# Moving one group's norm at the head of two context attentions, and adding their output biases batch by batch

## The chip, the cores and the metric

The kernel runs on one core of one Trainium2 chip. Its time is the device time of one launch in microseconds (us). An engine works through its instructions in the order in which the program gives them; work on one engine waits for work on another through semaphores. The engines are named as the profile names them: PE (matrix multiplications and transposes), PEld (its weight loads), DVE and POOL (element-wise work), ACT (activations and copies), SP (issues transfers, written SPq).

## The reference, cut to what matters

The reference is a decoder of four layers on 16 batches of 112 rows and 256 columns, in f32. Each layer is an attention, a context attention over 375 rows of context, and a feed-forward part, each with a layer norm ahead and a residual addition behind:

```python
x = x + _L2_attn_ref(_layernorm(x, axis=-1), ...)
x = x + _L2_xattn_ref(ctx_1024, _layernorm(x, axis=-1), mask_BxSxS2_ik0, ...)   # layer 3's context attention
x = x + _L2_ffn_ref(_layernorm(x, axis=-1), ...)                                # experts, two of eight for each row
x = x + _L3_attn_ref(_layernorm(x, axis=-1), ...)                               # a whole block: attention, norm, MLP
x = x + _L3_xattn_ref(_layernorm(x, axis=-1), ctx_1024, ctx_1024, ...)          # layer 4's context attention
x = x + _L3_ffn_ref(_layernorm(x, axis=-1), ...)                                # ternary weights
```

In the reference and in the kernel the layers count from 0, so `l2` in a name is layer 3 and `l3` is layer 4. Both context attentions have 16 heads of 16 columns: a query projection, scores against the keys of the context, a softmax, values, an output projection with a bias, and the residual. Layer 3's also norms its projected queries and keys and has a mask; layer 4's has neither. The feed-forward part of layer 4 (`l3f`) makes its two weights ternary at run time: the mean of the absolute values of each weight is formed, and each entry becomes −1, 0 or 1 by half that mean.

## The kernel before

The program runs twelve phases in order, `l0_attn` to `l3_ffn`. The residual lies on chip throughout, as the tile `xres` (`K.x`), 112 rows x 16 batches x 256. Batches are taken in four groups of four (`NG`, `G4`; `GC` is 448, the rows of one group). A framework allots the tiles, sets the semaphores and orders the instructions of each engine: near neighbours in the source may change places, and the order of issue on each engine is then fixed.

Many helpers are generators: a phase interleaves them step by step, so that the work of one fills the gaps of another. `zip_steps` runs several in turn until all have ended. `ln_steps` norms one group of four batches: statistics on DVE (lines 180, 181), variance plus epsilon (160), the reciprocal root on POOL (166, tiles `rs_...`), four row norms on DVE (207, tiles `xn_...`), eight transposes on PE (148, `lnT_...`) and two copies from PSUM to the transposed group `xT`.

Layer 3's context attention is `l2_xattn`. Ahead of it, in `l2_attn`, the norm of each group (`l2x_norm`) is made when its last batch is done; the fourth group's can only follow the last batch, whose last residual addition is POOL's line 1556. Then `l2_xattn` folds the value bias into the output bias (`add_output_bias`: two-chunk product `bo_l2x` on PE, sum `bc_L2x_bo` on DVE at 1007, 16 additions to the residual on POOL at 1009), scales `wo` (1676), fetches two batches (`fetch`: keys `kT`, values `v`, mask `mi`, all by SP) and projects them (`project`: `l2x_q` on PE, `qn` and its statistics on DVE, `rs_l2x_q` on POOL, `qp` on DVE at 1706, copies `vp` of the values on POOL at 1708, the mask row `neg` on DVE at 1710, four transposes `l2x_qT`). After that a stream runs over 64 units, a unit being a batch and four of its heads: scores `ha_sl2x` on PE, maxima `e` and `mx` on DVE (1733), exponentials on ACT, transposes `l2x_t`, and values `l2x_o` of the unit before. The projection of batch b+2 is spread over the stream as `ahead`, one step in each unit.

Layer 4's self-attention is `l3_attn`. Its tail is the MLP of the last group: norm `l3ac`, hidden `l3a_m` (32 matmuls), output `l3a_d` (64 matmuls), added to the residual at line 223. Only then `l3_xattn` begins with its own bias row (`bo_l3x`) and `queries(0)`, which norms group 0, adds the bias to its four batches on POOL (2172) and makes the projections `l3x_q`. `spread` copies the values of a batch on POOL (2166). The stream again takes four heads a step, t from −5 to 64: scores `ha_sl3x`, maxima `mx` (2192); a batch's maxima are turned (`shift`, `l3x_m`, sum `q` at 2240) ahead of the second product `l3x_t`, the exponentials `e` and the values `l3x_o`. `queries` of the next group is spread over the stream. The list `others` holds work of the phase after: `l3f_weights`, which loads `w_L3f_fc` and `w_L3f_proj` and makes them ternary on DVE (sums at 2280, tests `lo` at 2294, 2295), one step in each t from t = −5 on.

Other parts that the change touches: `open_nx` opens the pools `nx` (the tile `l2x_xT`, the transposed norm of a whole phase) and `so` (tiles for sorting rows by expert), which `program` closes after `l3_attn`. `Sorted` loads a table of constants (`sort_cols`) and is made twice, in `l1_ffn` and `l2_ffn`. The pool `w` has six slots for weights, used in turn; SP waits with a load for the slot's last reader.

Of the kernel before, what the change touches and what calls it, by code (L numbers as in the profile page):

```python
# [10 lines left out]
F32 = mybir.dt.float32  # L11
# [3 lines left out]
ALU = mybir.AluOpType  # L15
# [4 lines left out]
B = 16  # L20
S = 112
D = 256
T = B * S
# [3 lines left out]
G4 = 4  # L27
NG = B // G4
GC = G4 * S
# [12 lines left out]
class Kern:  # L42
# [33 lines left out]
    def open_nx(self):  # L76


        self.l3pools = [self.tc.tile_pool(name=n, bufs=1) for n in ("nx", "so")]
        nx, self.so_pool = [p.__enter__() for p in self.l3pools]  # L80
        self.l2x_xT = nx.tile([128, 2, T], F32, name="l2x_xT")
        self.normed = None

    def open_l3c(self):

        pools = [self.tc.tile_pool(name=n, bufs=m) for n, m in (("l3c1", 1), ("l3c", 2))]
        self.l3pools += pools
        w1, wk = [p.__enter__() for p in pools]
        steps = l3x_context(self, w1, wk)
        self.l3x_fill = lambda: next(steps, steps) is not steps  # L90

# [1086 lines left out]
class Sorted:  # L1178
# [4 lines left out]
    def __init__(self, K, pool, E, name):  # L1183
        self.K, self.E, self.name = K, E, name
        self.NT = (2 * T + E * 127) // 128
        self.xd = K.dram.tile([T, D], F32, name=f"{name}_xd")
        self.ys = K.dram.tile([self.NT * 128, D], F32, name=f"{name}_ys")
        self.shapes = pool.tile([128, K.ins["sort_cols"].shape[1]], F32, name=f"{name}_shapes")
        K.nc.sync.dma_start(out=self.shapes, in_=K.ins["sort_cols"])

    def shp(self, name):
        a, n = SORT_AT[name]
# [264 lines left out]
def l2_attn(K):  # L1457
# [3 lines left out]
    nc, tc = K.nc, K.tc  # L1461
# [3 lines left out]
    with tc.tile_pool(name="l2a", bufs=2) as wk, tc.tile_pool(name="l2a1", bufs=1) as w1:  # L1465
# [113 lines left out]
        while todo or live:  # L1579
            if todo:  # L1580
                b = todo.pop(0)
                if b % G4 == 0:
                    zip_steps(ahead)
                    ahead = scores(b // G4 + 1) if b // G4 + 1 < NG else iter(())
                live.append((b, attend(b)))
                if b % 2:
                    K.l3x_fill()
            for n, item in enumerate(list(live)):
                if next(item[1], item) is item:
                    live.remove(item)  # L1590
                    if item[0] % G4 == G4 - 1:
                        norms.append(K.l2x_norm(wk, item[0] // G4))
                if n % 2 == 0:
                    next(ahead, None)
            if norms and next(norms[0], norms) is norms:
                norms.pop(0)
# [57 lines left out]
def l2_xattn(K):  # L1654
# [4 lines left out]
    nc, tc = K.nc, K.tc  # L1659
    wq = K.weight("L2x_wq", 2, D)  # L1660
    wo = K.weight("L2x_wo", 2, D)
    with tc.tile_pool(name="l2x", bufs=2) as wk, tc.tile_pool(name="l2x1", bufs=1) as w1:
# [5 lines left out]
        qps = padded_tiles(K, w1, [S], "qp")  # L1668
        xT = K.l2x_xT
        if K.normed is None:  # L1670
            for q in range(NG):
                zip_steps(K.l2x_norm(wk, q))
        K.normed = None
        add_output_bias(K, wk, wo, K.col("L2x_vb"), K.brow("L2x_bo"), "l2x")
        for kk in range(2):
            nc.vector.tensor_scalar(wo[:, kk, :], wo[:, kk, :], K.col("L2x_vs")[:, kk : kk + 1], None, ALU.mult)
        bq = K.brow("L2x_bq")
        qs, qb = K.col("L2x_qs"), K.col("L2x_qb")
        ready, fetched = {}, {}

# [13 lines left out]
        def project(b):  # L1694
# [13 lines left out]
                nc.gpsimd.tensor_copy(vp[:, c, :, :16], v[:, c])  # L1708
            neg = wk.tile([S, SK], F32, tag="mask_f", bufs=3, name=f"neg{b}")
            nc.vector.tensor_scalar(neg, mi, 0.0, NEG, ALU.is_equal, ALU.mult)  # L1710
            if b + 1 < B and b > 0:
                fetch(b + 1)
            yield
# [57 lines left out]
        units = [(b, g) for b in range(B) for g in range(4)]  # L1771
        maxima, exponentials = scores(*units[0])
        exponentials(maxima())
        ahead, behind = iter(()), []
        for k in range(len(units) + 1):
            more = scores(*units[k + 1]) if k + 1 < len(units) else None
            if k:
                b, g = units[k - 1]
                values(b, g)
                if g == 2 and b + 2 < B:  # L1780
                    ahead = project(b + 2)
                if g == 3:
                    behind.append(heads_steps(K, wk, pos[b], wo, K.x[:, b, :], f"l2x{b}", True))
# [125 lines left out]
def l3_attn(K):  # L1909
# [5 lines left out]
    with tc.tile_pool(name="l3a", bufs=2) as wk, tc.tile_pool(name="l3a1", bufs=1) as w1:  # L1915
# [183 lines left out]
            mlp_step()  # L2099
        while outs:  # L2100
            out_steps()
        for g in mlps:
            zip_steps(g)

# [29 lines left out]
def l3_xattn(K):  # L2136
# [8 lines left out]
    with tc.tile_pool(name="l3x", bufs=2) as wk, tc.tile_pool(name="l3x1", bufs=1) as w1:  # L2145
# [20 lines left out]
                nc.gpsimd.tensor_copy(vps[b % 2][:, c, :, :16], vs[b][:, c])  # L2166

        def queries(q):
            xT = wk.tile([128, 2, GC], F32, tag="xT", name=f"xT{q}")
            yield from K.ln_steps(wk, K.x, q, "l3x", xT=xT, bufs=1)  # L2170
            for b in range(q * G4, (q + 1) * G4):
                nc.gpsimd.tensor_tensor(K.x[:, b, :], K.x[:, b, :], bo[:S], ALU.add)
            yield
            qTs[q] = wk.tile([128, 4, GC], F32, tag="qT", name=f"qT{q}")
            for g in range(4):
                ps = K.bank(f"l3x_q{q}{g}")
# [43 lines left out]
        for b in range(3):  # L2220
            fetch(b)
        bo = K.brow("L3x_bo")
        add_output_bias(K, wk, wo, K.col("L3x_bv"), bo, "l3x", ())
        zip_steps(queries(0))
        for b in range(2):
            spread(b)
# [1 line left out]
        for t in range(-5, 4 * B + 1):  # L2228
# [13 lines left out]
            for item in list(behind):  # L2242
                if next(item[1], item) is item:
                    behind.remove(item)
                    if item[0] % G4 == G4 - 1:
                        others.append(K.l3f_left.pop(0))
            if others and next(others[0], others) is others:
                others.pop(0)
            if 0 <= t < 4 * B and s < 3:
                weights(b, s)  # L2250
# [359 lines left out]
def program(tc, ins, out, phases):  # L2610
    with ExitStack() as ctx:
# [4 lines left out]
        for phase in phases:  # L2616
# [27 lines left out]
                    zip_steps(l3x_context(K, w1, wk))  # L2644
            if phase in (l3_xattn, l3_ffn) and not hasattr(K, "l3f_left"):
                pool = ctx.enter_context(tc.tile_pool(name="l3f1", bufs=1))
                K.l3f_xT = pool.tile([128, 2, T], F32, name="l3f_xT")
                K.l3f_left = [l3f_weights(K, pool)] + [l3f_rows(K, pool, q) for q in range(NG)]
            phase(K)
            if phase is l3_attn:  # L2650
# [22 lines left out]
```

## Time and profile before

| what | value |
|---|---|
| median of 3 runs | 3657.05 us (3647.51 to 3661.35) |
| profiled execution | 3657.38 us, of which the span of the trace is 3655.6 us |
| mean granted clock of PE | 0.941 of full speed |
| layer 3's context attention, last `l2a_y` on PE to first scores | 2098.9 to 2135.8 us |
| layer 4's context attention, end of `l3a_d` to first maximum | 3249.1 to 3269.4 us |

Times in the trace are us from the span's start. In a timeline a line gives the start, the length, the engine, the line of the kernel, the operation, output<-input and count; the bracket is the idle time of the engine just before, and who ended it. A line of waits gives the waiting engine and tile, who released it, the total, the number of times, and the longest. Where several like instructions follow each other they are merged in one line with their busy time. A window gives the busy time of each engine in a stretch, the granted clock of PE (1.00 is full speed), the share of the 16 transfer engines in use and GB/s.

### The profile page before, as it was taken

The page shows a single profiled execution, that of the slowest core. Times are in us where ns is not written, and L with a number is a line of the kernel's source. Part 1 is how long each engine was busy: PE and PEld are TensorE (multiplying, and loading weights), DVE is VectorE, ACT ScalarE, POOL GpSimd, SP SyncE. Part 2 cuts the span into 40 slices and gives each one's busy share as a digit, 9 for nine tenths or more (in the row PEclk, how much of TensorE's full clock was granted, in tenths as well). Part 3 has the DMA queues.
Part 4 walks back from the last instruction along what each step waited for, and adds up shares of the span by engine and source line. Part 5 has one row for each costly group of instructions (what it writes and reads, how often), then busy time and mean ns, then how long its engine had stood idle before and what let it go on. Part 6 is the DMA issues. An engine that isn't in the chain of part 4 may idle for free. (4 is left out here: it accounts for less than half of the span.)

```text
span 3655.6 us, 72104 instructions
## 1 busy us (share of the span) xinstructions
PE 3242.1 (89%) x29426; PEld 2225.4 (61%) x29426; DVE 1961.5 (54%) x5065; ACT 1343.8 (37%) x2772; POOL 481.3 (13%) x636
## 2 busy tenths in 40 slices
PE   5999989789988898689978979989999979889999
PEld 2444444456756676457664547668889856656666
DVE  5766665363264454445435568872442286457754
ACT  2344444332233233112233347742222246714431
POOL 1000000020110000020142420001000132022110
PEclk9999999999989888888999979998999989979999
DMA  3021211510131211314182122137999710021200
GB/s 124 22 51 30 62 44 35 106 47 18 41 94 46 71 48 44 90 31 126 61 288 79 47 66 57 41 96 276 355 355 308 244 40 1 1 66 47 55 6 21
DMA packets 231275, 332.48 MB, mean 91 GB/s; under 512 B 109904, under 2 KB 183728, under 8 KB 215840
## 3 DMA queue, kind: packets, MB, share of 16 engines
q1 hardware_dynamic: 207392, 295.22, 26.8%
q0 software_dynamic: 6816, 17.57, 1.8%
q10 hardware_dynamic: 16736, 15.07, 1.3%
q8 instruction: 232, 3.80, 0.4%
q14 instruction: 99, 0.81, 0.1%
HBM read 270.53 MB, written 57.27 MB: 90 GB/s over the span
## 5 line engine op out<-in xcount | busy, mean ns | idle before, releaser
L1842 DVE SCALAR_TENSOR_TENSOR hT<-l2f_b,b,sl 128x128 f32<-128x128 f32 x280 | 94.8, 349 | 248.6 <-PE l2f_b L154 121.1
L1841 ACT ACTIVATE sl<-l2f_a,b 128x128 f32<-128x128 f32 x280 | 98.9, 366 | 292.4 <-PE l2f_a L154 222.4
L154 PE MATMUL l2f_a<-l2f_xT,w_L2f_w 128*128 128x128 f32 x1120 | 194.8, 288 | 5.4 <-DMA w_L2f_w<-in_L2f_w 4.5
L154 PE MATMUL l2f_b<-l2f_xT,w_L2f_w 128*128 128x128 f32 x1120 | 188.2, 282 | 1.9 <-DVE hT L1842 1.1
L154 PE MATMUL l0x_k<-w_L0x_wk,cT 128*125 128x512 f32 x384 | 179.6, 611 | 0.0
L154 PEld LDWEIGHTS l2f_a<-l2f_xT,w_L2f_w 128*128 128x128 f32 x1120 | 161.3, 192 | 29.4 <-ACT sl L1841 12.5
L154 PE MATMUL l0x_c<-kn,cx 125*128 125x512 f32 x384 | 178.9, 603 | 0.0
L1742 ACT ACTIVATE e<-e,mx 112x375 f32<-112x375 f32 x256 | 143.1, 607 | 54.6 <-DVE mx L1737 54.6
L303 DVE TENSOR_TENSOR pr<-qT,kT 128x576 f32<-128x576 f32 (+14 forms) x168 | 145.6, 898 | 30.0 <-PE l0a_s L306 23.8
L154 PEld LDWEIGHTS l2f_b<-l2f_xT,w_L2f_w 128*128 128x128 f32 x1120 | 152.9, 192 | 5.6 <-DVE hT L1842 4.8
L2192 DVE TENSOR_REDUCE mx<-ha_sl3x 112x1 f32<-112x375 f32 x256 | 121.9, 537 | 51.8 <-PE ha_sl3x L1017 51.7
L154 PE MATMUL l2f_d<-w_L2f_w,hT 128*128 128x256 f32 x560 | 144.2, 380 | 0.0
L1733 DVE CUSTOM_DVE_ANT_0 e<-ha_sl2x,neg 112x375 f32<-112x375 f32 x256 | 125.0, 544 | 16.3 <-PE ha_sl2x L1017 14.2
L154 PEld LDWEIGHTS l0x_k<-w_L0x_wk,cT 128*125 128x125 f32 x384 | 71.4, 192 | 93.0 <-issue 87.5
L154 PEld LDWEIGHTS l0x_c<-kn,cx 125*128 125x128 f32 x384 | 70.0, 190 | 92.7 <-issue 88.3
L2212 ACT ACTIVATE e<-l3x_t 125x448 f32<-125x448 f32 x192 | 88.8, 551 | 96.4 <-PE l3x_t L2207 96.4
L411 ACT ACTIVATE sq_k<-l0x_k 125x512 f32<-125x512 f32 x96 | 57.3, 597 | 130.7 <-PE l0x_k L154 130.4
L154 PEld LDWEIGHTS l2f_d<-w_L2f_w,hT 128*128 128x128 f32 x560 | 95.7, 191 | 7.2
L306 PE MATMUL l0a_s<-pr,R 128*32 128x448 f32 x672 | 93.7, 547 | 6.7 <-DVE pr L303 6.6
L148 PE MATMUL l2x_t<-ident,e 112*125 112x112 f32 x768 | 97.6, 277 | 1.4 <-ACT e L1742 1.3
L148 PEld LDWEIGHTS l2x_t<-ident,e 112*125 112x125 f32 x768 | 93.3, 192 | 7.2 <-ACT e L1742 2.9
L154 PE MATMUL l2x_kv<-w_l2x_kv,ctxT 128*125 128x512 f32 x192 | 96.3, 655 | 0.0
(785 smaller groups left out, 7193.0 us busy)
## 6 DMA issues: line engine op xcount, KB each, us to landing
w_L2f_w<-in_L2f_w SPq DMA_DIRECT2D x105, 1024.0 KB
ctxT<-in_ctxT SPq DMA_DIRECT2D x48, 375.0 KB
w_L1f_e<-in_L1f_e SPq DMA_DIRECT2D x43, 384.0 KB
a<-skew SPq DMA_DIRECT2D x32, 392.0 KB
cx<-in_ctx SPq DMA_DIRECT2D x16, 375.0 KB
l2x_v<-vo SPq DMA_DIRECT2D x16, 375.0 KB
l2x_kT<-kTo SPq DMA_DIRECT2D x16, 375.0 KB
c<-in_ctx SPq DMA_DIRECT2D x16, 375.0 KB
```

What stands on the lines that cost most here:

```text
L148: self.nc.tensor.transpose(out, in_, self.ident[:k, :k])
L154: self.nc.tensor.matmul(out, lhsT=l, rhs=r, start=i == 0, stop=i == n - 1)
L303: V.tensor_tensor(prs[j][:, :, :, off:], qT[q][:, :, :, off:], kT[q][:, :, :, : S - off], ALU.mult)
L306: nc.tensor.matmul(ps[32 * j : 32 * j + 32, :GC], lhsT=R[:, hf, 4 * c + j, x, :], rhs=prs[j][:, hf].rearrange("p b s -> p (b s)"), start=x ...
L411: nc.scalar.activation(sq[:p, n * 8 : n * 8 + 8, :], heads[n], AF.Square)
L1733: nc.vector.tensor_tensor_reduce(out=e[:, j, :], in0=banks[j][:S, :SK], in1=neg, scale=1.0, scalar=-3.0e38, op0=ALU.add, op1=ALU.max, accu ...
L1742: nc.scalar.activation(es[b, g][:, j, :], es[b, g][:, j, :], AF.Exp, bias=mx[:, 1, j : j + 1], scale=0.25)
L1841: nc.scalar.activation(sl, pa[:, at], AF.Silu, bias=b1[:, m + i : m + i + 1])
L1842: nc.vector.scalar_tensor_tensor(hT[:, m + i, :], pb[:, at], b1[:, 8 + m + i : 9 + m + i], sl, ALU.add, ALU.mult)
L2192: nc.vector.tensor_reduce(mxs[b][:, 4 * g + j : 4 * g + j + 1], ps[:S, :SK], AX.X, ALU.max)
L2212: nc.scalar.activation(es[b, c][:, j].rearrange("p g s -> p (g s)"), banks[j][:CK, :GC], AF.Exp, scale=0.25)
```

## The change

In layer 3 the norm of groups 0 to 2 stays in `l2_attn`; group 3's is made in the stream of `l2_xattn`, as the first `ahead`, with its row norms in a slot of the pool `w`. `add_output_bias` and the scaling of `wo` stand behind the first unit's scores; the bias is added there for batches 0 and 1 only, and for later ones in `project`.

In layer 4 the norm of group 0 is made at the end of `l3_attn`, interleaved with the last MLP block, into the first part of `l2x_xT`; `queries(0)` takes it from there. Its bias row is formed at t = −3, together with the additions to batches 0 to 3. The work in `others` begins at t = 0. The pools `nx` and `so` stay open to the end, `l3f_xT` is the same tile as `l2x_xT`, and the sorting table is loaded once.

```diff
@@ open_nx
-        self.l3pools = [self.tc.tile_pool(name=n, bufs=1) for n in ("nx", "so")]
-        nx, self.so_pool = [p.__enter__() for p in self.l3pools]
+        nx, self.so_pool = [self.ctx.enter_context(self.tc.tile_pool(name=n, bufs=1)) for n in ("nx", "so")]
@@ open_l3c
-        pools = [self.tc.tile_pool(name=n, bufs=m) for n, m in (("l3c1", 1), ("l3c", 2))]
-        self.l3pools += pools
-        w1, wk = [p.__enter__() for p in pools]
+        self.l3pools = [self.tc.tile_pool(name=n, bufs=m) for n, m in (("l3c1", 1), ("l3c", 2))]
+        w1, wk = [p.__enter__() for p in self.l3pools]
@@ Sorted.__init__
-        self.shapes = pool.tile([128, K.ins["sort_cols"].shape[1]], F32, name=f"{name}_shapes")
-        K.nc.sync.dma_start(out=self.shapes, in_=K.ins["sort_cols"])
+        if not hasattr(K, "sort_shapes"):
+            K.sort_shapes = pool.tile([128, K.ins["sort_cols"].shape[1]], F32, name="sort_shapes")
+            K.nc.sync.dma_start(out=K.sort_shapes, in_=K.ins["sort_cols"])
+        self.shapes = K.sort_shapes
@@ l2_attn
-                    if item[0] % G4 == G4 - 1:
+                    if item[0] % G4 == G4 - 1 and item[0] < B - 1:
                         norms.append(K.l2x_norm(wk, item[0] // G4))
@@ l2_xattn
-            for q in range(NG):
+            for q in range(NG - 1):
                 zip_steps(K.l2x_norm(wk, q))
         K.normed = None
-        add_output_bias(K, wk, wo, K.col("L2x_vb"), K.brow("L2x_bo"), "l2x")
-        for kk in range(2):
-            nc.vector.tensor_scalar(wo[:, kk, :], wo[:, kk, :], K.col("L2x_vs")[:, kk : kk + 1], None, ALU.mult)
-        bq = K.brow("L2x_bq")
+        bo, bq = K.brow("L2x_bo"), K.brow("L2x_bq")
@@ l2_xattn, project
             nc.vector.tensor_scalar(neg, mi, 0.0, NEG, ALU.is_equal, ALU.mult)
+            if b > 1:
+                nc.gpsimd.tensor_tensor(K.x[:, b, :], K.x[:, b, :], bo[:S], ALU.add)
@@ l2_xattn, stream
         exponentials(maxima())
-        ahead, behind = iter(()), []
+        add_output_bias(K, wk, wo, K.col("L2x_vb"), bo, "l2x", range(2))
+        for kk in range(2):
+            nc.vector.tensor_scalar(wo[:, kk, :], wo[:, kk, :], K.col("L2x_vs")[:, kk : kk + 1], None, ALU.mult)
+        rows = K.w_pool.tile([128, 2048], F32, tag="w", name="l2x_rows")[:S, : G4 * D].rearrange("p (b d) -> p b d", b=G4)
+        ahead, behind = K.ln_steps(wk, K.x, NG - 1, "l2x", xT=xT[:, :, (NG - 1) * GC :], nat=rows), []
...
                 if g == 2 and b + 2 < B:
+                    zip_steps(ahead)
                     ahead = project(b + 2)
@@ l3_attn, end
-        for g in mlps:
-            zip_steps(g)
+        xT = K.l2x_xT.rearrange("p k t -> p (k t)")[:, : 2 * GC].rearrange("p (k s) -> p k s", k=2)
+        zip_steps(*mlps, K.ln_steps(wk, K.x, 0, "l3x", xT=xT))
+        K.l3x_first = xT
@@ l3_xattn, queries
-            xT = wk.tile([128, 2, GC], F32, tag="xT", name=f"xT{q}")
-            yield from K.ln_steps(wk, K.x, q, "l3x", xT=xT, bufs=1)
-            for b in range(q * G4, (q + 1) * G4):
-                nc.gpsimd.tensor_tensor(K.x[:, b, :], K.x[:, b, :], bo[:S], ALU.add)
-            yield
+            if q == 0 and hasattr(K, "l3x_first"):
+                xT = K.l3x_first
+            else:
+                xT = wk.tile([128, 2, GC], F32, tag="xT", bufs=1, name=f"xT{q}")
+                yield from K.ln_steps(wk, K.x, q, "l3x", xT=xT, bufs=1)
+            if q:
+                for b in range(q * G4, (q + 1) * G4):
+                    nc.gpsimd.tensor_tensor(K.x[:, b, :], K.x[:, b, :], bo[:S], ALU.add)
+                yield
@@ l3_xattn
         bo = K.brow("L3x_bo")
-        add_output_bias(K, wk, wo, K.col("L3x_bv"), bo, "l3x", ())
         zip_steps(queries(0))
@@ l3_xattn, stream
-            if others and next(others[0], others) is others:
+            if t == -3:
+                add_output_bias(K, wk, wo, K.col("L3x_bv"), bo, "l3x", range(G4))
+            if t >= 0 and others and next(others[0], others) is others:
                 others.pop(0)
@@ program
-                K.l3f_xT = pool.tile([128, 2, T], F32, name="l3f_xT")
+                K.l3f_xT = K.l2x_xT if hasattr(K, "l2x_xT") else pool.tile([128, 2, T], F32, name="l3f_xT")
```

## The prediction

> **What bounds the kernel now.** I read the page first, then the waits and timelines of the two places the change touches, then their windows. The page:
>
> ```profile
> span 3655.6 us, 72104 instructions
> ...
> PE 3242.1 (89%) x29426; PEld 2225.4 (61%) x29426; DVE 1961.5 (54%) x5065; ACT 1343.8 (37%) x2772; POOL 481.3 (13%) x636
> ```
>
> [...] The instruction counts on PE, DVE, ACT and POOL stay the same here; only places change. The profiled execution took 3657.38 us (span 3655.6 plus 1.8 around it), 0.3 above the median 3657.05; the sum is made against it.
>
> Waits at the head of layer 3's context attention (2098 to 2140 us):
>
> ```profile
> PE l2x_qT L148 <- DVE qp L1706: 13.8, 2, 11.0
> ...
> PE lnT_l2x L148 <- DVE xn_l2x L207: 13.3, 1, 13.3
> DVE qp L1706 <- POOL rs_l2x_q L166: 5.9, 2, 5.2
> ...
> DVE neg L1710 <- DMA mi<-in_mask: 3.1, 1, 3.1
> ```
>
> Columns: total wait, times, longest. PE loses 27.1 us here: to group 3's norm, and to the first batch's query norm, whose rstd stands on POOL behind the 16 bias additions (POOL's timeline: start, length):
>
> ```profile
> 2117.11 11.08 POOL L1009 TENSOR_TENSOR xres<-xres,bc_L2x_bo 112x256 f32<-112x256 f32 x16 [5.51 <-DVE bc_L2x_bo L1007]
> 2128.16 0.54 POOL L166 TENSOR_TENSOR rs_l2x_q<-ve_l2x_q,mhalf 112x1 f32<-112x1 f32 x1
> ```
>
> The head of layer 4's (PE):
>
> ```profile
> 3235.09 13.98 PE L2031 MATMUL l3a_d<-l3w_cm,mT 128*112 128x256 f32 x64
> 3249.99 1.09 PE L154 MATMUL bo_l3x<-w_L3x_wo,bvb_l3x 128*112 128x256 f32 x4 [0.92 <-PE l3a_d L2031]
> 3254.41 1.75 PE L148 MATMUL lnT_l3x<-ident,xn_l3x 112*128 112x112 f32 x8 [3.33 <-DVE xn_l3x L207]
> 3256.72 9.23 PE L154 MATMUL l3x_q<-xT,w_L3x_wq 128*128 128x448 f32 x16 [0.56 <-ACT xT L136]
> ```
>
> Bias, norm, then projections; the scores follow at 3265.9. Their maxima come later, since DVE stands before them on group 1's norm, whose rstd is on POOL behind copies that wait for `v`:
>
> ```profile
> 3264.75 2.20 DVE L207 TENSOR_SCALAR xn_l3x<-xres,mv_l3x,rs_l3x 112x256 f32<-112x256 f32 x4 [7.06 <-POOL rs_l3x L166]
> ...
> 3269.36 4.17 DVE L2192 TENSOR_REDUCE mx<-ha_sl3x 112x1 f32<-112x375 f32 x9
> ```
>
> The windows show who binds afterwards (length, then PE, PEld, DVE, ACT, POOL busy, clock, DMA):
>
> ```profile
> 2137.00:2150.00 13.00, 11.73 (x63) 6.82 (x57) 7.97 (x31) 5.21 (x11) 0.00 (x0) 0.50 0.14 44
> 2150.00:2200.00 50.00, 48.58 (x587) 34.78 (x586) 44.06 (x153) 38.95 (x82) 4.94 (x12) 1.00 0.29 64
> ...
> 3270.00:3296.00 26.00, 23.09 (x226) 16.89 (x230) 25.73 (x59) 5.33 (x12) 1.54 (x3) 0.55 0.11 41
> 3296.00:3320.00 24.00, 23.96 (x353) 14.50 (x354) 16.48 (x37) 12.08 (x25) 4.38 (x9) 1.00 0.27 63
> ```
>
> Layer 3's stream starts PE-bound at half clock, then runs with PE full and DVE at 88%. Layer 4's starts DVE-bound (25.73 of 26) and turns PE-bound.
>
> **Layer 3's head.** By the changed order PE goes from the last `l2a_y` (2098.9) straight to the projection `l2x_q` of batch 0, since group 3's columns are no longer wanted first. On DVE `qn` waits for POOL's last residual addition, which ends at 2109.6 (L1556, 2108.89 and 0.72 long). Its statistics and variance take 0.43 + 0.18 + 0.15, rstd 0.54 and `qp` 0.46, with hops: `qp` is done at about 2112.4, against 2129.2 now. `v` and the mask of batch 0 are issued when that addition ends, too (now 2114.2, after the norm); the mask lands 8.5 us behind `v`'s issue (2114.22 to 2122.7), so at 2118.2. In DVE's new order `neg` stands ahead of batch 1's variance: `ve` about 2119.0, rstd 0.54, `qp` 2120.0 to 2120.8, four transposes, first scores at 2121.8 (now 2135.8). Ahead of the first maximum DVE also does group 3's statistics and two of its four row norms (0.35 each): 2123.7 against 2137.4. **Gain 13.7.**
>
> What left the head comes back in the stream: `bo_l2x` (four matmuls, 2.02 us at half clock, 1.09 at the clock of layer 4's `bo_l3x`) and eight `lnT_l2x` (1.89 at half clock, about 1.0 at full). PE is full there, so I charge 3.0, between 2.1 and 3.9. DVE's extra (two row norms, 0.70, two `wo` scalings, 0.70, bias row 0.42) falls where DVE has 7.97 of 13 us: nothing; without that cover 1.8. Beside busy POOL an SBUF operation of DVE is longer: `neg` took 0.82 at 2122.7 against a usual 0.35, so four or five of these could pay 0.5 each, 2.3 in all, still inside DVE's 5 us of slack. [...]
>
> POOL: the additions now stand behind batch 1's rstd and ahead of the copies `vp` of batch 1; they start when the bias row is ready (about 2126.7) and end 11.1 us later, the copies at 2139. They are wanted at `l2x_o` of batch 1, now 2162.7, then 2148.7, and batch 2's rstd (now 2158.6, then 2144.6) has 5 us to spare: nothing; if POOL's additions took 1.2 instead of 0.69 us, the cover would be gone and each further us counts. SP: `v` of batch 4 waits for those copies, two batches early: nothing. **Net −10.7**, from −14 (everything hidden) to −8 (the mask 3 us later, all of the extra charged).
>
> The shift passes on: in the stream PE and DVE are both nearly full, and the transfers of layer 3's experts start only after its routing, so behind it.
>
> **Layer 4's head.** Group 0's norm goes into the last MLP block of layer 4's self-attention: four row norms on DVE (1.38) ahead of the copy that releases `l3a_m`, eight transposes on PE, of which DVE's 1.4 and half a us of PE's come ahead of the matmuls: the end of `l3a_d` (now 3249.07) moves to about 3251.0, +1.9. Then `l3x_q` follows without a gap, and at full clock: its last banks took 1.5 us each against 3.4 and 2.9 for the first two after the idle, so 6.1 instead of 9.23. On POOL group 1's rstd is now ahead of the copies of `v`, so DVE's norms run through. The first maximum comes about 8.0 us behind `l3a_d`, at 3259.0 instead of 3269.4: 10.4 us sooner.
>
> Not all lasts. In DVE's new order four sums of `w_L3f_fc` and three of `w_L3f_proj` stand ahead of the maxima of batch 1's third head group. DVE reaches the latter 14.5 us behind its first maximum (24 maxima at 0.45, four sums at 0.6, three small ones, 1.2), at 3273.5. SP now issues `v` of batch 4 ahead of `w_L3f_proj`. Each `v` runs at 125 GB/s (the windows 3270 to 3276 show a DMA share of a third), 3 us; in the trace this queue is empty at 3278.5, 29.4 behind `l3a_d`'s end. So `w_L3f_proj` lands 25 to 29 us behind it, 3276 to 3280, and DVE stands 2.5 to 6.5. From there three sums, four maxima and a fourth sum (4.5 us) bring the last head group's maxima of batch 1 to 3280.5 to 3284.6, now 3292.4: **−7.8 to −11.9, I take −9**, nearer to the late landing, as the queue is in order. The ternary work on `w_L3f_fc` (four of 0.43 and four of 0.72 us, 4.6), now in the DVE-bound stretch, moves into the PE-bound stream. The same burst for `w_L3f_proj` cost PE an idle of 2.6 (3321 to 3325): +2.6, from 0 (in gaps) to 4.6 (all). **Net −6.4**, from −3 to −11.9. The bias additions of group 0 by batch are off every path, as POOL is busy 4.4 of 24 us there.
>
> **The rest.** One copy of the sorting table (0.2 MB) is loaded instead of two, a small weight's load (`L2f_wr`) comes later though hundreds of us early, `l3f_xT` takes over a buffer that is read out by then, the memset of ones and a copy come sooner on POOL: nothing each, at most 1 together. Sum −10.7 − 6.4 = −17.1, 3640.3 us: about 3640.
>
> **The rivals.**
> (a) Clock stays up in layer 4. After an idle of only 2.39 (3267.6 to 3269.95) the clock was 0.50 to 3284 and 0.55 over 3270 to 3296, though PE was busy 23.09 of 26. If group 0's scores now come without such a gap, the chain from 3286.7 to 3293.8 (`l3x_t` 2.47 against 1.07, `l3x_o` 1.65 against 0.90, scores 1.54 against 0.83, `lnT` 1.43 against 0.75) is 3.5 us shorter: with the forecast's other terms 3637, with a shorter `w_L3f_proj` wait too 3633. Against it: DVE still feeds the first scores, at 0.45 a bank. [...]
> (b) Layer 4 gives nothing: `w_L3f_proj` at 29 us and the burst in full, and `fc` late by 2 as well. Only layer 3 is left, −8 to −11: 3648.
> (c) Layer 3's head doesn't get its mask sooner. If `mi` lands when it does now (2122.7), because the queue and not the issue sets it, 4.5 of 13.7 are gone: 3645.
> (d) The other side: DVE's in-order wait on `w_L3f_proj`. Its place is ahead of the maxima of batch 1's third head group; each us of landing later is one on the path. Layer 4 is no better than before from a landing at about 3288 (37 behind `l3a_d`), and layer 3's gain is used up from 3299; it would take a queue twice as slow as the 29.4 us seen. At 3310, 3668.
>
> **How the numbers follow.** Forecast 0.42, (a) 0.20, (b) 0.17, (c) 0.13, (d) 0.08. What a measurement can tell from no change is 0.5%, 18.3 us, so 3638.8 is the border and the forecast lies 1 us inside it. The terms' bounds give 3632 to 3646 for the forecast; somewhat over half of it, and all of (a), is faster: 0.43. (b), (c), the rest of the forecast and the mild part of (d): within, 0.52; the rest of (d) slower, 0.05. Range 3627 (both heads at their best) to 3652 (only the low end of layer 3).
>
> **What would show it.** Right: `l2x_q` directly behind `l2a_y`; one PE wait of 13 us gone, the first `ha_sl2x` 12 to 14 us sooner relative to `l2a_y`, `rs_l2x_q` ahead of the additions on POOL; `l3x_q` near 6 us, the first `mx` 8 us behind `l3a_d`; a DVE wait on `w_L3f_proj` of 2 to 6. Wrong: first scores of layer 3 bound to the mask at 2122, POOL's additions delaying `vp`, PE idle of more than 5 us around the `w_L3f_fc` burst, or a DMA wait on `w_L3f_proj` over 10.

## The result, and the profile after

The changed kernel took 3633.02 us (median of 4 runs, 3628.32 to 3639.81) against 3657.05: a ratio of 0.9946, 95% interval 0.9923 to 0.9969. A later comparison gave 0.9941 (0.9921 to 0.9962, e0 below). (The medians lie 24.0 us apart, which alone would be 0.9934; the interval belongs to the ratio, so the text goes by the ratio.) So it is faster by 0.54 to 0.59%, some 20 us of 3657, and the interval reaches to both sides of the 0.5% that the prediction took as its border. The profiled execution was the slowest of the four: 3639.81 us with a span of 3638.0, against 3657.38 and 3655.6 before.

How long the program takes to reach layer 3's context attention differs by up to 29 us from run to run, whatever the kernel (the last `l2a_y` starts between 2098.5 and 2127.6). Kernels are therefore compared stage by stage. The four stages that the change can touch, in us, worked out from the first and the last start of each tile's matmuls on PE in the profiled execution of each kernel (the end of a matmul is modelled in the trace). A head runs up to the first scores or values, a stream from there to the last values:

```
                                 layer 3 head     layer 3 stream    layer 4 head     layer 4 stream    sum
                                 last l2a_y to    to the last       last l3a_d to    to the last
                                 first ha_sl2x    l2x_o             first l3x_o      l3x_o
before                               37.3             273.6             40.4             232.1        583.4
changed                              21.3             271.3             34.8             234.9        562.3
e0  changed, once more               21.5             271.5             33.9             235.5        562.4
e1  layer 3's part alone             22.5             272.2             39.7             237.8        572.2
e2  layer 4's part alone             35.2             273.9             34.2             232.4        575.7
e3  pools, table, buffer alone       36.9             274.3             40.3             232.1        583.6
e6  changed, bias at the head        30.3             274.9             34.9             233.6        573.7
e7  changed, norm at the head        26.4             272.2             34.4             232.4        565.4
e11 changed, bias row later          22.4             285.5             34.9             233.7        576.5
e8  changed, ternary from t = -5     19.8             273.9             33.1             235.7        562.5
e4  changed, early weights           20.8             272.1             24.7             233.6        551.2
e5  before, early weights            37.2             273.7             37.1             232.0        580.0
e10 e4 and a free first slot         17.4             271.3             25.0             233.6        547.3
e12 before, with filler              37.5             269.8             40.6             232.0        579.9
```

From before to changed the four stages lose 21.1 us. The profiled executions differ by 17.6 only, because what lies outside these stages came out 3.5 longer in this one. Most of it, 3.2, lies between the last `l2x_o` and layer 3's first expert, where the code is the same and which takes 76.7 to 80.9 us among these kernels; 0.6 lies between the first and the last `l3a_d`, where group 0's norm now stands, and the rest is 0.3 shorter.

**Layer 3's head.** The waits of the changed kernel from 2098 to 2122 us (total, times, longest):

```profile
PE l2x_qT L146 <- DVE qp L1703: 16.4, 2, 11.6
...
DVE qn L1699 <- POOL xres L1556: 3.0, 1, 3.0
...
DVE neg L1707 <- DMA mi<-in_mask: 1.5, 1, 1.5
...
DVE qp L1703 <- POOL rs_l2x_q L164: 1.2, 2, 0.9
```

PE's wait of 13.3 on the norm `xn_l2x` is gone, its wait for `qp` grew from 13.8 to 16.4, and DVE's wait for the rstd fell from 5.9 to 1.2 us. The timeline of PE there:

```profile
2099.33 1.03 PE L152 MATMUL l2x_q<-w_L2x_wq,l2x_xT 128*112 128x256 f32 x4
2112.01 1.01 PE L146 MATMUL l2x_qT<-ident,qp 112*128 112x112 f32 x4 [11.65 <-DVE qp L1703]
2112.81 1.91 PE L152 MATMUL l2x_q<-w_L2x_wq,l2x_xT 128*112 128x256 f32 x4
2119.46 1.01 PE L146 MATMUL l2x_qT<-ident,qp 112*128 112x112 f32 x4 [4.73 <-DVE qp L1703]
2120.39 1.61 PE L1015 MATMUL ha_sl2x<-kT,qT 32*112 32x375 f32 x8
2121.93 2.05 PE L152 MATMUL bo_l2x<-w_L2x_wo,bvb_l2x 128*112 128x256 f32 x4
2123.91 1.15 PE L1015 MATMUL ha_sl2x<-kT,qT 32*112 32x375 f32 x8
```

`l2x_q` stands directly behind `l2a_y`, and `bo_l2x` lies between the scores of the first and the second unit. On POOL, the rstd of both batches is ahead of the additions, and the next rstd has some time to spare behind them:

```profile
2118.40 0.56 POOL L164 TENSOR_TENSOR rs_l2x_q<-ve_l2x_q,mhalf 112x1 f32<-112x1 f32 x1
...
2125.05 1.46 POOL L1007 TENSOR_TENSOR xres<-xres,bc_L2x_bo 112x256 f32<-112x256 f32 x2 [3.73 <-DVE bc_L2x_bo L1005]
2126.46 9.83 POOL L1709 TENSOR_TENSOR xres<-xres,bc_L2x_bo 112x256 f32<-112x256 f32 x14
2136.22 1.10 POOL L1705 COPY vp<-v 125x256 f32<-125x256 f32 x3
2140.74 0.55 POOL L164 TENSOR_TENSOR rs_l2x_q<-ve_l2x_q,mhalf 112x1 f32<-112x1 f32 x1 [3.42 <-DVE ve_l2x_q L158]
```

**Layer 4's head.** PE, and then DVE, in the changed kernel:

```profile
3220.18 13.98 PE L2035 MATMUL l3a_d<-l3w_cm,mT 128*112 128x256 f32 x64
3234.00 6.18 PE L152 MATMUL l3x_q<-l2x_xT,w_L3x_wq 128*128 128x448 f32 x16
...
3258.36 2.04 PE L2217 MATMUL l3x_t<-q,kT 32*125 32x112 f32 x32 [6.07 <-DVE q L2249]
...
3266.64 2.03 PE L2217 MATMUL l3x_t<-q,kT 32*125 32x112 f32 x30 [4.62 <-DVE mx L2202]
3268.60 1.72 PE L1023 MATMUL l3x_o<-e,vp 125*32 125x112 f32 x32
```

```profile
3241.89 0.52 DVE L2202 TENSOR_REDUCE mx<-ha_sl3x 112x1 f32<-112x375 f32 x1
...
3256.19 0.69 DVE L2291 TENSOR_REDUCE sm_L3f_fc<-w_L3f_fc 128x4 f32<-128x512 f32 x1 [5.19 <-DMA w_L3f_fc<-in_L3f_fc]
3256.79 0.99 DVE L2202 TENSOR_REDUCE mx<-ha_sl3x 112x1 f32<-112x375 f32 x2
3257.70 0.61 DVE L2249 TENSOR_TENSOR q<-qT,l3x_m 128x448 f32<-128x448 f32 x1
...
3264.19 0.69 DVE L2291 TENSOR_REDUCE sm_L3f_proj<-w_L3f_proj 128x4 f32<-128x512 f32 x1 [2.27 <-DMA w_L3f_proj<-in_L3f_proj]
```

The projections follow `l3a_d` without a gap and at full clock (1.00 from 3234.0 to 3240.2), and the first maximum comes 7.7 us behind its end (3234.16 to 3241.89; before 20.3). Then DVE stands twice in front of a weight that has not landed: 5.19 us for `w_L3f_fc`, 2.27 for `w_L3f_proj`. The sum `q` of the first batch is queued behind the first of these, and with it `l3x_t` and the values.

The windows that answer to those of before (length, PE, PEld, DVE, ACT, POOL busy, clock, DMA share, GB/s), each beginning within a microsecond of the same distance behind its first scores or its first maximum:

```profile
2121.60:2134.60 13.00, 11.87 (x114) 7.28 (x111) 12.65 (x47) 8.05 (x17) 9.55 (x14) 0.89 0.28 88
2134.60:2184.60 50.00, 48.96 (x585) 34.86 (x584) 44.97 (x156) 38.32 (x81) 7.65 (x18) 1.00 0.33 79
3242.00:3268.00 26.00, 13.46 (x106) 8.33 (x109) 18.50 (x41) 2.00 (x5) 9.57 (x16) 0.67 0.40 129
3268.00:3292.00 24.00, 23.10 (x322) 14.18 (x318) 18.03 (x41) 11.01 (x22) 4.58 (x8) 0.93 0.14 34
```

Two things are new. Layer 3's stream starts at a clock of 0.89 instead of 0.50, with DVE busy for 12.65 of 13 us instead of 7.97. And layer 4's first 26 us, where DVE was busy for 25.73, now have it at 18.50, and the two waits of 5.19 and 2.27 are the other 7.5: the stretch is no longer bound by DVE's work but by the arrival of weights.

### The profile page after: what moved, and what is told of

Same layout as the page of the kernel before. It is cut to its first block, busy times and chain, and to the rows that moved or that the text cites. A ratio compares the mean times of both kernels' runs of the same rounds, so it can differ in the third digit from the quotient of the medians.

```text
span 3638.0 us, 72110 instructions
## 1 busy us (share of the span) xinstructions
PE 3243.1 (89%) x29426; PEld 2231.0 (61%) x29426; DVE 1962.6 (54%) x5065; ACT 1343.9 (37%) x2772; POOL 479.8 (13%) x636
```

## The experiments

Theory: layer 3's head gives most, as group 3's norm and the bias additions no longer stand ahead of the first scores; layer 4's head gives less than its sooner start, since DVE waits in order on the weights of the last phase. Rivals: other stages carry the difference; or layer 4's rest is set by something else than these loads. e5, e6, e7, e8, e11 and e12 have one run each and are read by their stages alone.

**e0, e1, e2, e3: the parts apart.** e0 is the changed kernel once more. e1 is the kernel before with the hunks of `l2_attn` and `l2_xattn` only; e2 is it with the hunks of `l3_attn` and `l3_xattn`, the pools, the table and the shared buffer; e3 with the pools, the table and the shared buffer only:

```diff
-        self.l3pools = [self.tc.tile_pool(name=n, bufs=1) for n in ("nx", "so")]
-        nx, self.so_pool = [p.__enter__() for p in self.l3pools]
+        nx, self.so_pool = [self.ctx.enter_context(self.tc.tile_pool(name=n, bufs=1)) for n in ("nx", "so")]
...
-                K.l3f_xT = pool.tile([128, 2, T], F32, name="l3f_xT")
+                K.l3f_xT = K.l2x_xT if hasattr(K, "l2x_xT") else pool.tile([128, 2, T], F32, name="l3f_xT")
```

> The changed kernel again, beside the runs that follow. From the first two traces: last l2a_y to first scores of layer 3 21 us (before 37), first scores to last l2x_o 271 to 274 either way, last l2x_o to first l2f_a 80 (before 77), l3a_d to first scores of layer 4 6.3 (before 17.2), from there to the first l3x_o 28 (before 23). 0.4 to 0.7% below the kernel before.

> The kernel before with the change in layer 3 alone (group 3's norm in the stream, bias behind the first scores). Theory A (the gain is the two heads, each by its own waits, and adds up): the first scores of layer 3 come 14 to 15.5 us sooner after the last l2a_y, as in the changed kernel, and the whole is 11 to 14 us faster (3643 to 3646 against 3657); the head of layer 4 keeps its first maximum 20 us behind l3a_d. Theory B (part of the gain is in the placing of tiles and the shared tables): less than 9 us, since those parts are missing here.

> The kernel before with the change in layer 4 and with the shared pools, table and l3f_xT, without the change in layer 3. Theory A: 4 to 8 us faster (3649 to 3653), with the DVE waits on w_L3f_fc (5 us) and w_L3f_proj (2 us) of the changed kernel. Theory B: more than 10 us faster.

> The kernel before with only the pools kept open, the sorting table loaded once and l3f_xT sharing the tile of l2x_xT (and one buffer instead of two for xT in layer 4's context attention, for space). Theory A: within 2 us of the kernel before. Theory B: 4 us or more faster.

Against the kernel before: e0 0.9941 (0.9921 to 0.9962); e1 0.9954 (0.9933 to 0.9974), 3652.83 against 3666.21 us; e2 0.9992 (0.9972 to 1.0011); e3 1.0005 (0.9986 to 1.0025). Layer 3's part carries the gain and layer 4's is within its interval of nothing, at a middle of −3 us (from −10 to +4), short of the 4 to 8 us that it was expected to gain; the two middles add up to −0.54%, the whole. The stages say the same with less scatter. e1's layer 3 is as in the changed kernel (22.5 and 272.2), its layer 4 head as before (39.7); e2 is the mirror image (35.2 and 273.9; 34.2). e3 leaves every stage as it was. The one stage that does not follow its part is layer 4's stream: 237.8 in e1, whose code there is that of before. It scatters by several us, and the 2.8 us between before and changed can't be read from one pair.

**e6, e7: one half of layer 3's head put back.** e6 has the bias row, the scaling and 12 additions ahead of the first scores again, e7 has group 3's norm in `l2_attn` again:

```diff
+        add_output_bias(K, wk, wo, K.col("L2x_vb"), bo, "l2x", range(B - G4))
...
-            if b > 1:
+            if b >= B - G4:
```

```diff
-                    if item[0] % G4 == G4 - 1 and item[0] < B - 1:
+                    if item[0] % G4 == G4 - 1:
```

> The changed kernel, with layer 3's bias row and the additions to batches 0 to 11 back ahead of the first scores (12 additions on POOL; the last four stay in the stream, since group 3 is normed there). If the additions ahead of rs_l2x_q are half of what the head lost: first scores 27 us behind the last l2a_y, 6 more than in the changed kernel. If the norm alone mattered: 21 to 23.

> The changed kernel, with group 3's norm back in layer 3's self-attention, ahead of the first projection; the bias stays behind the first scores. If each of the two waits is paid by itself: first scores 26 to 28 us behind the last l2a_y. If the additions alone mattered: 21 to 23.

The head came out at 30.3 us with the bias (27 was expected) and 26.4 with the norm (26 to 28), against 21.3 with neither and 37.3 with both. So the bias costs 9.0 and the norm 5.1, 14.1 of the 16.0 when each is put back alone; the remaining 2 are no more than the scatter of this stage, which takes 19.8 to 22.5 us in the six kernels that have its changed code. In e6 the first rstd stands behind the additions (8.24 us long) as it did before, and PE waits 9.11 us for `qp`; in e7 PE waits 12.13 for `xn_l2x`, but 2.68 for the `qp` that follows.

**e4, e5, e8: the wait on the weights in layer 4.** (The expectation of e5 says layer 3's context attention; the loads stand in `l3_xattn`, layer 4's.) e4 is the changed kernel, and e5 the kernel before, with both weights loaded at the start of `l3_xattn`, ahead of its own loads, so that in e4 `w_L3f_fc` is issued 15 us ahead of the end of `l3a_d` instead of 3 behind it and the sums fall into idle time of DVE in the MLP; e8 is the changed kernel without its `t >= 0`:

```diff
+    K.l3f_pre = {"L3f_fc": K.weight("L3f_fc", 2, 1024), "L3f_proj": K.weight("L3f_proj", 8, D)}
...
-        w = K.weight(name, k, n)
+        w = K.l3f_pre[name]
```

```diff
-            if t >= 0 and others and next(others[0], others) is others:
+            if others and next(others[0], others) is others:
```

> The changed kernel, with w_L3f_fc and w_L3f_proj loaded at the start of layer 4's context attention, ahead of its keys and values and so during the MLP before. Theory A: the two DVE waits (5.2 and 2.3 us) go, the sums too move to where DVE is idle (8 of 0.6 us), so layer 4's head is 9 to 12 us shorter than in the changed kernel and the whole that much faster: 3621 to 3625. Rival C: the half clock of PE or the landing of the values sets this stretch as soon as DVE does not wait; then 0 to 5 us.

> The kernel before, with `w_L3f_fc` and `w_L3f_proj` loaded at the start of layer 3's context attention, as in the run with early weights of the changed kernel. Theory that the early load pays only because the changed order puts the sums ahead of maxima that could otherwise run, while the kernel before had no wait of DVE on these weights: last `l3a_d` to first `l3x_o` is 38 to 41 us (now 40.4), total within 3 us of the kernel before. Rival (the load itself, or the sums' place in the stream, costs the kernel before as much as the changed one): 30 to 33 us, total 8 to 10 us less.

> The changed kernel, with the ternary work of the last phase begun at t = -5 again instead of t = 0. Theory that what holds the first values is DVE's place behind the sum of `w_L3f_fc`, which lands 22 us behind `l3a_d`: the sums stand earlier on DVE, ahead of more maxima, and the same landing stops more work, so last `l3a_d` to first `l3x_o` grows from 34.3 us to 36 to 42. Rival (the wait costs nothing of its own, DVE's amount of work ahead of the first values sets the time): within 1 us of 34.3, or by the 4.6 us of ternary work moved ahead, with no wait on `w_L3f_fc` longer than 5.2.

e4: 3634.52 us, 0.9914 of the kernel before (0.9881 to 0.9946). Its layer 4 head takes 24.7 us, 10.1 less than the changed kernel's, as expected. The 3621 to 3625 us expected for the whole were meant beside a kernel before of 3657, which took 3666.21 beside e4; by the ratios e4 lies 10 to 12 us under the changed kernel. PE there:

```profile
3256.68 2.04 PE L2218 MATMUL l3x_t<-q,kT 32*125 32x112 f32 x32 [0.39 <-DVE q L2250]
...
3262.99 1.72 PE L1023 MATMUL l3x_o<-e,vp 125*32 125x112 f32 x32
```

The waits of 6.07 and 4.62 ahead of the two `l3x_t`, 10.7 together, are down to 0.39 and 0.50. So the late weights and their sums held back 10 us of what the sooner start had to give.

In e5 the same edit gave the kernel before 3.3 us (40.4 to 37.1): a little more than the theory's 38 to 41, far from its rival's 30 to 33. The kernel before had no wait on these weights, but its four sums of `w_L3f_fc`, 2.7 us, stood between the maxima; that these are the 3.3 is not shown. The early load is worth 10 us only where the scores start early.

In e8 the sums stand ahead of more maxima, and I had expected 36 to 42 us; measured were 33.1, 1.2 less than the middle of the changed kernels' and nearest to the rival. DVE waits 4.98 us for `w_L3f_fc`, which lands 22.0 us behind `l3a_d`, as in the changed kernel (5.19, 22.0). By either order the first `q` comes when that weight has landed, 24.7 us behind `l3a_d` in e8 and 23.5 in the changed kernel. What e8 loses there it gets back at `w_L3f_proj`: its first sum comes 27.8 us behind `l3a_d` without a wait, where the changed kernel waits until 30.0. So beginning the ternary work only at t = 0 gained nothing that shows here.

**e11, e12: the clock at the start of layer 3's stream.** The stream came out 2.3 us shorter than before although it had got work. Its clock had come back sooner, and I suspected the place of `bo_l2x`: in the kernel before PE has an idle of 1.27 us there, at the first exponentials, while in the changed kernel the product lies ahead of the second scores. e11 takes `bo_l2x` out of that place (`add_output_bias` and the scaling three units later); e12 is the kernel before with the same product made once more just there, unused, and nothing else:

```diff
+            if k == 2:
+                add_output_bias(K, wk, wo, K.col("L2x_vb"), bo, "l2x", range(2))
```

```diff
         exponentials(maxima())
+        again = wk.tile([128, 2, S], F32, tag="bv_b", bufs=1, name="again")
+        nc.vector.tensor_copy(again, bcast(K.col("L2x_vb"), 2, S))
+        ps = K.bank("again_l2x")
+        K.mm(ps[:S, :D], [(again[:, kk, :], wo[:, kk, :]) for kk in range(2)])
+        nc.vector.tensor_copy(again[:S, 0, :8], ps[:S, :8])
```

> The changed kernel with the bias row of layer 3 (product `bo_l2x`, sum, additions for batches 0 and 1) and the scaling of `wo` three units later in the stream, behind the fourth unit's scores instead of the first's. The place where PE had an idle of 1.3 to 2 us in the kernel before (behind the first three head groups' scores, at the first exponentials) is then not filled by `bo_l2x`. Theory that `bo_l2x` fills this gap and so brings PE's clock back sooner: the granted clock is back at full 12 to 15 us behind the first scores, as in the kernel before, instead of 4 to 6; first scores to last `l2x_o` 273.5 to 275 us instead of 271.3; total 2 to 3 us over the changed kernel. Rival (what counts is that PE's idle ahead of the scores is shorter in the changed kernel, not the gap): clock back at 4 to 6 us, 271 to 272 us. By both the head, last `l2a_y` to first scores, stays 21 to 21.7 us.

> The kernel before, with nothing moved and work added: behind the first unit's scores the bias product of layer 3 is made once more (four matmuls on PE, two small copies on DVE), its result unused, so that PE has the same work as in the changed kernel between the first and the second unit's scores. Theory that work in this gap keeps PE from the idle that holds the clock down: the granted clock is back at full 4 to 7 us behind the first scores instead of 14, first scores to last `l2x_o` 271 to 272.5 us instead of 273.6, in spite of the added work; a drop back within the next microseconds, as in the run with the ternary work from the start, would leave the 273.6. Rival (the gap does not matter, the changed kernel's earlier clock comes from its shorter idle ahead of the scores or from other moved work): clock back at 12 to 16 us, 274 to 276 us. By both the head stays 37.3 us.

e12 answers for the place. Its head is 37.5 us, as before, its stream 269.8 instead of 273.6, with more work in it and below the 271 to 272.5 expected. (Its total, one run of 3673.80 against 3667.49, says nothing at this size.) In PE's timeline the second scores follow the filler at once, and the windows show the clock at full from 4 us behind the first scores on:

```profile
2152.25 1.60 PE L1017 MATMUL ha_sl2x<-kT,qT 32*112 32x375 f32 x8
2153.79 2.05 PE L154 MATMUL again_l2x<-w_L2x_wo,again 128*112 128x256 f32 x4
2155.77 1.09 PE L1017 MATMUL ha_sl2x<-kT,qT 32*112 32x375 f32 x8
```

```profile
2154.30:2156.30 2.00, 2.00 (x8) 1.08 (x10) 1.97 (x11) 0.00 (x0) 0.00 (x0) 0.52 0.00 0
2156.30:2158.30 2.00, 1.58 (x11) 0.55 (x3) 1.49 (x9) 1.96 (x4) 0.00 (x0) 1.00 0.48 118
```

The other kernels agree. With no product at this place the clock is back at full 14.2 to 15.6 us behind the first scores (before, e2, e3, e5, e6, e11); with it, after 3.0 to 5.7 us (changed, e0, e1, e4, e7, e8, e10, e12), though e7 and e8 lose it again until 10.1 and 13.2. e6, whose stream has less work than the changed kernel's but no product there, takes 274.9. The sizes fit: as an estimate, 10.2 us less at half clock are worth up to 5.1 us of PE's work, the filled idle 1.27, the product costs 2.05, together 4.3 against the measured 3.8. That it is the idle which held the clock is not shown by this; see the last section.

The kernel before, 4 us and 14 us behind its first scores:

```profile
2139.80:2141.80 2.00, 0.94 (x3) 0.73 (x4) 1.93 (x10) 1.60 (x4) 0.00 (x0) 0.50 0.50 119
...
2149.80:2151.80 2.00, 2.00 (x28) 1.35 (x31) 0.70 (x2) 1.91 (x4) 0.00 (x0) 0.96 0.00 0
```

In e11 PE idles 1.96 us at this place and the clock comes back some 15 us behind the first scores, as the theory said. The stream of 285.5 us was 11 beyond its 273.5 to 275. The timelines of POOL, DVE and PE show another cause in it:

```profile
2155.50 9.73 POOL L1709 TENSOR_TENSOR xres<-xres,bc_L2x_bo 112x256 f32<-112x256 f32 x14
2165.19 0.54 POOL L164 TENSOR_TENSOR rs_l2x_q<-ve_l2x_q,mhalf 112x1 f32<-112x1 f32 x1
```

```profile
2165.77 0.46 DVE L1703 TENSOR_SCALAR qp<-qn,mv_l2x_q,rs_l2x_q 112x256 f32<-112x256 f32 x1 [4.76 <-POOL rs_l2x_q L164]
```

```profile
2166.75 2.99 PE L1015 MATMUL ha_sl2x<-kT,qT 32*112 32x375 f32 x8 [2.97 <-DVE mx L1732]
```

The bias row came later and POOL's additions with it, so that batch 2's rstd stood behind them: DVE stopped for 4.76 us, PE for 2.97, and the 20 us around this (2154.7 to 2174.7) have a clock of 0.83, the next 20 one of 0.91. That this makes the whole of the 11 us is not shown. In the changed kernel the same rstd has 3.42 us to spare. This is the cover that the prediction named for the additions, used up.

**e10: both heads.** e4, and the projected queries, their statistics and the first mask of batches 0 and 1 in a slot of the weights' pool, whose earlier readers are long done:

```diff
+        first = K.w_pool.tile([128, 2048], F32, tag="w", name="l2x_first")
...
+            if b == 0:
+                mi = first.bitcast(I32)[:S, 512 : 512 + SK]
...
-            qn = wk.tile([S, D], F32, tag="qn", name=f"qn{b}")
+            qn = first[:S, b * D : (b + 1) * D] if b < 2 else wk.tile([S, D], F32, tag="qn", name=f"qn{b}")
```

> The changed kernel with the early loads of w_L3f_fc and w_L3f_proj, and with the query rows, statistics and mask of layer 3's first batches in a free slot of the weights' pool. Theory A (in the changed kernel qn waits for POOL's last addition and the mask's load is late only because their buffers lie in space that the attention before still uses): the first scores of layer 3 come 16 to 17 us behind the last l2a_y instead of 21, and the whole is 4 us below the version with the early loads alone, 14 below the changed kernel. Rival: the chain through group 3's rows on DVE and POOL sets the first scores; then 20 us or more.

3646.89 us against 3689.45, 0.9893 (0.9867 to 0.9919). The head is 17.4 us, 4 less than the changed kernel's, just beyond the 16 to 17 expected and far from the rival's 20; PE's first wait for `qp` is 5.85 instead of 11.65, the second 5.52 instead of 4.73. So half of the first wait, and 5 us of the 16.4 in all, came from where these tiles lie, not from what they need: `qn` had waited for POOL's last addition (3.0 us), whose operands are other tiles. With layer 4's 25.0 this is the best version, 1.07% under the kernel before.

## Why the prediction was right

The 3640.0 us forecast, with −17.1, stands against a median of 3633.0 and −21 in the four stages: 3633 is inside the range, and the change is faster. That the sum fits so well is in part luck, as it came out right by two errors against each other. Layer 3 gave 6.5 us more than forecast, layer 4 some 3 less. The means below are over the kernels of the table that have the stage as it was before and as it is in the changed kernel, e11's stream aside.

- **Layer 3's head: right, 14.0 forecast.** Measured 15.4 (means 36.8 and 21.4). In the profiled execution the first scores came at 2120.4, forecast for 2121.8; `qp` was done at 2111.95, forecast for 2112.4, and the mask landed at 2117.82, forecast for 2118.2. `qn` did wait for POOL's last addition. Rival (c) falls with the mask.
- **The charge of +3.0 in layer 3's stream: wrong in sign, and the term that failed.** The stream became 1.8 us shorter (means 273.9 and 272.1). e12, one trace, puts the credit that I had left out at 4.1 us against the 273.9, net of the product's own 2.05: with the product at this place PE's clock came back 10.2 us sooner (4.0 us behind the first scores instead of 14.2). What was moved beside it, above all the eight `lnT_l2x` charged at 1.0 to 1.9, cost about 1.5 to 2.4 (269.8 to 271.3 and 272.2). e8, with the same code in layer 3, bounds the credit from the other side: there the clock was at full from 3 us behind the first scores on, fell again from 6 to 13 us, behind a window in which PE idled for 1.03 of 2 us, and the stream took 273.9, as before. I had seen the half clock in the window of before and took it for a property of the place; it was one of what PE did there.
- **POOL's additions cost nothing: right**, with 3.4 us of cover where I had said 5, and e11 shows what lies beyond it.
- **Layer 4's sooner start: right.** `l3x_q` 6.18 us (6.1), first maximum 7.7 behind `l3a_d` (8.0). From the first to the last `l3a_d` it takes 0.5 us longer (medians 193.0 and 193.5 us), where 1.9 was forecast: 1.4 in favour.
- **What lasts of it: mis-sized.** I took −9 at the last maxima of batch 1 and put DVE's wait on `w_L3f_proj`, at 2.5 to 6.5 us. Those maxima came at 3271.69, 37.5 behind `l3a_d`, where they had been 43.3: with the 0.5, −5.3. The term that was missing is the wait for `w_L3f_fc`, 5.2 us, which the forecast counted as landed: in the kernel before its first sum found it there 24.4 us behind `l3a_d`, but in the new order DVE asks for it at 16.8 and it lands at 22.0. `w_L3f_proj` then took 2.3 more. The first values came 5.7 us sooner (means 40.3 and 34.5). e4 shows that the two together held 10 us.
- **The burst of +2.6: not shown.** Layer 4's stream is 1.7 us longer on the mean of the six changed kernels than the 232.1 of before, but from 0.3 to 3.4, and e1 has 5.7 with the code of before. Net of layer 4: −5.7 + 0.5 + 1.7 = −3.5 against −6.4; e2's middle of −3 agrees.
- **The rest at nothing: right** (e3).

Rival (a) fell: the window behind the first maximum shows a clock of 0.67, with PE's waits of 6.07 and 4.62 in it. In e4, without these waits, the clock still went to half 16.6 us behind `l3a_d`, for 10.2 us. Rival (b), layer 4 at nothing, had a wait on `fc` in it; the −3.5 lies about midway between it and the forecast, but the total went the other way because of layer 3. Rival (d) had the right mechanism on the other side: an in-order wait of DVE on a weight. Its two waits are 7.5 us and could not have brought a loss, as the landing, 22 and 30 us behind `l3a_d`, is far from its 37.

## What to carry to other kernels

When a stage starts sooner, ask what lands next at the old time: here two weights of a later phase, in front of which an engine stood in order. Issuing their loads some 18 us earlier was worth more in that head (10.1 us) than the rest of the edit (5.7), and little without it (3.3). Work moved off a head may be worth placing into a gap of PE on purpose: in e12 2.05 us of added work there made the stream 3.8 us shorter, with the clock back 10 us sooner. And a wait on an operation that reads none of the waiting tile's data can be a matter of where the tile lies: the 3.0 us of `qn` behind POOL's last addition were gone in e10, which gave it another slot.

## What was not expected of the hardware

With one short gap behind the first scores PE's clock came back some 10 us later than without it (14.2 us behind them in the kernel before, 4.0 in e12). From the start of the second `l2x_qT`, PE ran without a gap and was at full clock after 5.0 us in the changed kernel (2119.46 to 2124.47) and after 4.9 in e12 (2151.32 to 2156.21); among the eight kernels with the product at this place it is 3.9 to 6.7. With one idle of 1.27 us in the kernel before, which ends at 2140.86, the clock came back only at 2149.96, after another 9.1 us of work without a gap. In e8 a full clock was lost again around an idle of 0.75 us, 1.03 us in its window:

```profile
2133.60:2135.60 2.00, 0.97 (x7) 0.42 (x3) 2.00 (x9) 1.71 (x4) 1.34 (x2) 1.00 0.34 103
2135.60:2137.60 2.00, 1.86 (x8) 1.69 (x9) 1.66 (x7) 1.32 (x3) 2.00 (x4) 0.61 0.29 103
2137.60:2139.60 2.00, 2.00 (x12) 0.87 (x10) 1.12 (x2) 1.70 (x4) 2.00 (x4) 0.50 0.07 27
```

PE is busy again for 1.86 and 2.00 of 2 us while the clock goes down. Why the 9.1 us without a gap did not bring the clock back sooner, where 4.9 and 5.0 were enough, and why it fell around an idle as short as 0.75, is not shown by these runs.

The idle may not be what holds the clock. The product that brings it back runs over 128 rows, while scores run over 32, and the kernel before has a stretch in layer 4's head where PE makes scores alone for 7.18 us without a gap (24 `ha_sl3x` from 3269.95 on) and stays at half clock:

```profile
3270.00:3272.00 2.00, 2.00 (x8) 1.95 (x10) 2.00 (x5) 0.00 (x0) 0.60 (x1) 0.50 0.33 133
3272.00:3274.00 2.00, 2.00 (x12) 1.96 (x10) 2.00 (x5) 0.00 (x0) 0.00 (x0) 0.50 0.31 125
3274.00:3276.00 2.00, 2.00 (x10) 1.35 (x7) 2.00 (x5) 0.00 (x0) 0.00 (x0) 0.50 0.33 131
```

The same holds at the place in question: in the 3.9 us from the first scores on PE is busy for 3.82 us in the kernel before, with scores alone, and for all 3.9 in e12, with the product between. At their end the clock rises in e12 and not in the kernel before, whose idle has hardly begun. No run puts scores into the gap, or leaves the gap and changes the work ahead of it. So that the product at this place brings the clock back is shown, whether by filling the gap or by its kind is not.
